# Deformable convolution on one core: x loads on SyncE, statistics from band 4 on, one of four tile copies by a transfer, another order of stores and loads at the head

## The chip, the cores and the metric

The kernel runs on one core of one Trainium2 chip. The metric is the device time of one execution in microseconds (us), the median of several runs. The engines are named as in the profile: PE is TensorE, DVE is VectorE, ACT is ScalarE, POOL is GpSimd, SP is SyncE, which here only issues transfers (DMAs). ACT, POOL and SP each have their own queue of transfers.

## The reference, cut to what matters

The input x is 8 samples x 128 channels x 64 x 64. Layer 0 adds to x a deformable 3x3 convolution of its group-normalised copy (each of 9 taps reads the image at a position shifted by a learned offset, bilinearly, times a sigmoid mask), followed by batch normalisation over all samples and a relu. Layer 1 adds a mixture of four 3x3 convolutions, of which each sample chooses two, and a shared one. The change lies in layer 0 alone.

```python
om  = conv3x3(gn(x), off_w) + off_b            # 27 planes: 9 y offsets, 9 x offsets, 9 masks
val = bilinear(gn(x), grid + off) * sigmoid(om[:, 18:])
y   = einsum('bckhw,ock->bohw', val, w) + b    # 9 taps, 128 channels
x   = x + relu(batchnorm(y) * gamma + beta)
...
x   = x + moe_conv3x3(gn(x), top-2 of 4 experts) + shared_conv3x3(gn(x))
```

## The kernel before, in words

**Sampling as matmuls.** Every sample is cut into 8 horizontal bands of 8 rows (NB = 8); band g = 8b + j is band j of sample b, 64 bands in all. Inside a band the pixels are gathered in small tiles of 4 columns, and the samples at the shifted positions are made by TensorE: a tile of pixels (transposed, `xt`) times a sparse weight matrix s. An element of s is a tent in x times a tent in y, so `weights(n)` (L846) makes s on VectorE as a product of a table of x weights (`xwts`) and a table of y weights (`ywts`). The numbers of s run on: n = 5g + q, with five sample groups q a band.

**The tables.** For every sample `tables(b)` makes, from the statistics of the image (`statistics`, eight `bn_stats`, L303), the normalised image (`pad`, L343 on ACT and L347 on DVE), the offset convolution (combinations of rows in the combo buffers, L421 and L423, and matmuls, L456), the offsets in rows and columns through HBM (stores L523 and L530, loads L568 and L554), tents on ACT (L639, L643), masks on DVE (L676), and tables of x distances and y weights that are stored to HBM (`store_x` L594, `store_y` L666). It is a generator: each call of `tick()` puts the next few instructions into the program, and `pause(n)` lets n ticks pass. So the table work for sample b+2 is woven, tick by tick, into the bands of samples b and b+1. Statistics run in band 5 of sample b (`j == NB - 3`), the tables start there at tap 7, the combos fall in bands 6 to 0, the offsets are loaded and turned into tents in bands 1 to 4.

**One band** (the loop over g):
- For q = 0 to 4: `weights` for the group three ahead (AHEAD = 3), then `sample`: 12 matmuls into PSUM (L862) and one copy by ACT (L872). So in q = 0 the fourth s of the same band is made, in q = 1 the fifth, in q = 2 to 4 the first three of the next band. With q = 2 and 3 POOL issues the eight y loads of band g+2 (L725), which wait for the last s that read the buffer.
- Then the nine taps ("parts" 0 to 8) of the convolution of band g-1 (L911), with other work between them: at parts 0 and 1 transposes for band g+2 (L807, ACT copies L810); at part 2 the x load of band g+3 (two transfers of 576 KB together, L744, on POOL); at parts 1, 3, 5 and 7 `spread` of band g+2, which turns x distances into weights: absolute values on ACT (L763, L766) at parts 1 and 3, clips on DVE (L769) at parts 5 and 7; at part 4 `pick` for g+3 (L778).
- `share` (L821) copies the transposed tiles of band g+2 shifted by one for the other parity, in four pieces of 32 rows: pieces 0 and 2 by DVE at parts 2 and 3, pieces 1 and 3 by ACT at parts 4 and 6. So the tiles of a band are made two bands ahead.
- `put_off` adds after the second group the statistics of y (L991) and copies at the edge (L888 to L895).

**What orders the work.** Instructions of one engine run in program order. PE, DVE, ACT, POOL and SP wait for each other only where data or a buffer asks for it: `xwts` has three buffers, `ywts` two, s four, the PSUM tiles pq three, and the tiles pt, pm, pv and pc share one PSUM buffer.

**The head.** Sample 0's tables are made before the first band; they end with the stores of x distances and y weights, the loads for band 0, the statistics of sample 1 and the first spread.

The loop around the change:

```python
made, means_of = later, iter(())
...
if odd == 0 and part == 2:
    load_x(g + 3, nc.gpsimd)
...
if odd == 0 and part in (2, 3, 4, 6):
    piece = {2: 0, 3: 2, 4: 1, 6: 3}[part]
    share(g + 2, piece, MOVES[piece])
```

Of the kernel before, what the change touches and what calls it, by code (L numbers as in the profile page):

```python
# [17 lines left out]
H = W = 64  # L18
# [22 lines left out]
NR = 2 * REACH + 1  # L41
T = 4
# [3 lines left out]
NROW = H // T  # L46
NB = NROW // 2
# [18 lines left out]
def deform_moe_conv(  # L66
# [113 lines left out]
    def dense():  # L180

        with ExitStack() as st:
# [126 lines left out]
            def tables(b):  # L309
# [233 lines left out]
                )  # L543
                yield from pause(16)
                by_row = rowwise[b].rearrange("(t k u) h w -> k h t u w", t=3, k=3)
# [31 lines left out]
                if b == 0:  # L577
                    for piece in range(4):
                        share(1, piece, MOVES[piece])
                yield from pause((50, 9)[b] if b < 2 else 35)  # L580

# [114 lines left out]
                distances_x()  # L696
                store_x(0, 2, nc.gpsimd)
                load_x(0, nc.gpsimd)
                for i in (0, 1, 2):
# [6 lines left out]
                for k in range(Q):  # L706
                    for h in range(2):
                        load_y(0, k, (nc.sync, nc.gpsimd, nc.scalar, nc.gpsimd)[k % 4], (h,))
                for _ in statistics(1):
                    pass  # L710
                for tiles in ((NCOL, NCOL + 1), (0, 3), (3, 9), (9, NCOL)):
                    spread(0, tiles)
                store_x(2, 6, nc.gpsimd)
                store_x(6, NROW, nc.sync)
                store_y(0, NR, slice(4 * T, H))

# [108 lines left out]

            MOVES = (nc.vector.tensor_copy, nc.scalar.copy) * 2

            def width(q):
                return GT * T + 2 * (q in (0, NGR - 1))

            def weights(n, engine=nc.vector):

                if n >= len(bands) * NGR:
                    return
                g, q = divmod(n, NGR)
                s = a6.tile([P, M, 3 * (GT * T + 2)], F32, name="s")
                by_x = x_wts[g % 3].rearrange("p (c m x) -> p m c x", m=M, x=3)
                by_y = y_wts[g % 2].rearrange("p r y w x -> p (r y) w x")
                main = GT * T * q
                parts = [(2 * (q == 0), main, 2 + main, GT * T)]  # L840
                if q == 0:
                    parts.append((0, NCOL * T, 0, 2))
                if q == NGR - 1:
                    parts.append((GT * T, NCOL * T + 2, W - 2, 2))
                for at, c, w, k in parts:
                    engine.tensor_tensor(  # L846
                        s[:, :, 3 * at : 3 * (at + k)].rearrange("p m (c x) -> p m c x", x=3),
                        by_x[:, :, c : c + k], by_y[:, :, w : w + k], ALU.mult,
                    )
                ss[n] = s  # L850
# [114 lines left out]
            for n in range(AHEAD):  # L965
                weights(n, nc.vector if n < AHEAD - 1 else nc.gpsimd)
            HALVES = (0, EVEN), (EVEN, NCOL + 1)
# [32 lines left out]
            for g in range(len(bands) + 1):  # L1000
                b, j = bands[g] if g < len(bands) else (B, 0)
                if j == NB - 3:
                    means_of = statistics(b + 2)
# [3 lines left out]
                for q in range(NGR):  # L1007
                    if g < len(bands):
                        if g or q + AHEAD < NGR:
                            weights(g * NGR + q + AHEAD)  # L1010
                        sample(g * NGR + q)
                        if q in (2, 3):
                            for k in range(T * (q - 2), T * (q - 1)):
                                load_y(g + 2, k, nc.gpsimd)
                    if g == 0 and q == 1:
                        for _ in range(2):
                            while next(later) != BLOCK:
                                pass
                        for _ in range(8):
                            next(later)  # L1020
                    if q == 1:
                        put_off()
                taps = conv(g - 1) if g else iter(())
                twice = 2 if g and bands[g - 1][1] == NB - 1 else 1
                for done, _ in enumerate(taps):
                    part, odd = divmod(done, twice)
                    if odd == 0 and part in PIXELS:
                        next(turned, None)
                    if odd == 0 and part == 2:
                        load_x(g + 3, nc.gpsimd)  # L1030
                    if odd == 0 and part in SPREAD:
# [29 lines left out]
                if g == 0:  # L1061
                    for piece in range(4):
                        share(2, piece, MOVES[piece])
                    load_x(3, nc.gpsimd)
                    pick(3)
# [3 lines left out]
                    spread(2)  # L1069
                if g == 4:  # L1070
                    quad_weights()
# [603 lines left out]
```

## Time and profile before

| what | value |
|---|---|
| median of 3 runs | 1478.61 us (1473.09 to 1479.34) |
| the profiled execution | 1472.76 us, span 1471.0 us |
| mean granted TensorE clock | 0.96 |
| PE busy | 1300.3 us (88% of the span) |
| DVE busy | 1064.9 us (72%) |
| ACT busy | 902.7 us (61%) |
| POOL busy | 448.5 us (30%) |
| software DMA queue (POOL's) | 137.50 MB, 44.6% of the 16 engines' span |
| hardware DMA queue (SP's and ACT's) | 87.97 MB, 20.4% |

Layer 0 takes about the first 1085 us of the span. In the profile a row of a group is: line, engine, operation, output <- inputs, sizes, count, busy time, mean duration, and the idle time just before with what ended it. In a timeline a row is start, busy time, engine, line, operation; a bracket at its end is the idle time before it and its releaser. In a table of windows the columns are the window, its length, busy time (and count) of PE, PEld, DVE, ACT, POOL, the granted clock (PEclk), the share of the DMA engines and GB/s. Where bands are named below, a band begins with its first sample matmul and ends with the next band's.

Lengths of bands, read from the PE timeline in this way (us):

| sample | band 4 | band 5 | band 6 | band 7 | band 0 of the next |
|---|---|---|---|---|---|
| 1 | 18.6 | 16.1 | 13.1 | 17.2 | 21.0 |
| 2 | 17.5 | 17.9 | 13.1 | 17.2 | 21.9 |
| 3 | 14.7 | 18.5 | 14.7 | 17.2 | 21.1 |
| 4 | 18.9 | 17.9 | 13.1 | 17.2 | 21.0 |
| 5 | 21.8 | 17.9 | 13.1 | 17.2 | 21.1 |
| 6 | 13.9 | 14.9 | 13.1 | 13.1 | 18.6 |

Bands 1 to 3 of these samples take 12.2 to 13.1 us. Sample 0 is longer: its bands 0 to 7 take 17.2, 24.9, 23.4, 14.1, 13.1, 26.6, 14.8 and 30.0 us.

### The profile page before, as it was taken

What the parts mean: (1) busy time and instruction counts of PE and PEld (TensorE: products, weight loads), DVE (VectorE), ACT (ScalarE), POOL (GpSimd) and SP (SyncE); (2) the same over time, 40 slices, a digit from 0 to 9 for tenths busy, and PEclk for the clock granted to TensorE, in tenths of its full rate; (3) what the DMA queues carried; (4) which work ended last, traced back from release to release, by engine and by line L of the source; (5) the groups of instructions that cost most, each with busy time, mean ns of one, the idle gap of its engine ahead of it and who ended that gap; (6) DMA issues with size and microseconds to landing.
All of it is one profiled execution on the core that took longest, in us unless ns stands there. A gap on an engine that the chain in (4) does not pass through costs nothing.

```text
span 1471.0 us, 21219 instructions
## 1 busy us (share of the span) xinstructions
PE 1300.3 (88%) x7561; PEld 740.1 (50%) x7561; DVE 1064.9 (72%) x2113; ACT 902.7 (61%) x1183; POOL 448.5 (30%) x755
## 2 busy tenths in 40 slices
PE   4169779989989998998998999989975999999998
PEld 1144446555655665664565566556642444444443
DVE  5657687689668868967875896756628877878882
ACT  2365766887787688689777868977723333231320
POOL 6353232343343343343343334344212101011000
PEclk9579989999999999999999999999997999999999
DMA  4485755976887598598778778777618544565411
GB/s 147 106 184 122 164 131 133 208 180 140 182 184 181 129 211 186 126 189 182 171 145 174 179 168 170 174 194 181 175 32 243 140 120 135 149 171 158 114 44 60
DMA packets 146342, 227.33 MB, mean 155 GB/s; under 512 B 100574, under 2 KB 103802, under 8 KB 135986
## 3 DMA queue, kind: packets, MB, share of 16 engines
q0 software_dynamic: 79472, 137.50, 44.6%
q1 hardware_dynamic: 66618, 87.97, 20.4%
q8 instruction: 62, 1.02, 0.3%
q14 instruction: 54, 0.44, 0.1%
q10 hardware_dynamic: 136, 0.41, 0.1%
HBM read 180.23 MB, written 45.35 MB: 153 GB/s over the span
## 4 chain that ended last, share of the span: by engine, by line
PE 46%; DMA 16%; DVE 15%; issue 10%; ACT 9%; POOL 3%; SPq 1%; DVEq 0%; ACTq 0%; POOLq 0%
PE py L911 16%; PE pc L1587 14%; PE pq L862 10%; DMA ywts<-taby 5%; DMA xwts<-tabx 4%; DVE s L846 3%; PE pt L807 2%; PE pc L456 2%; DVE combo L423 2%; ACT xwts L763 2%; DVE stats L303 2%; POOL ywts L725 2%; DVE xwts L769 2%; DVE combo L421 1%; DMA pad<-in_x_dram 1%
## 5 line engine op out<-in xcount | busy, mean ns | idle before, releaser
L911 PE MATMUL py<-samples,dw_sb 128*128 128x512 f32 (+3 forms) x1296 | 553.4, 561 | 7.2 <-ACT y L919 5.4
L725 POOL DMA_DIRECT2D ywts<-taby x512 | 296.6, 600 | 527.3 <-DVE s L846 440.9
L862 PE MATMUL pq<-s,xt 64*128 64x144 f32 (+1 forms) x3840 | 294.1, 307 | 90.8 <-DVE s L846 50.6
L862 PEld LDWEIGHTS pq<-s,xt 64*128 64x128 f32 x3840 | 264.5, 195 | 136.0 <-ACT samples L872 55.3
L911 PEld LDWEIGHTS py<-samples,dw_sb 128*128 128x128 f32 x1296 | 228.2, 189 | 206.7 <-issue 178.1
L872 ACT COPY samples<-pq 128x864 f32<-128x864 f32 (+1 forms) x320 | 282.5, 972 | 53.0 <-PE pq L862 52.1
L846 DVE TENSOR_TENSOR s<-xwts,ywts 128x72 f32<-128x72 f32 (+1 forms) x447 | 199.5, 500 | 68.6 <-PE pq L862 59.2
L1587 PE MATMUL pc<-v,u 128*128 128x512 f32 x384 | 174.2, 600 | 6.3 <-DVE v L1494 6.3
L1587 PE MATMUL pc<-v,wmix 128*128 128x512 f32 x384 | 173.2, 596 | 0.0
L763 ACT ACTIVATE xwts<-xwts,place 128x1152 f32<-128x1152 f32 (+3 forms) x132 | 153.0, 1163 | 23.4 <-DMA xwts<-tabx 21.5
L821 DVE COPY xt<-xt 32x896 f32<-32x896 f32 x126 | 78.5, 623 | 114.2 <-ACT xt L810 113.2
L1565 ACT ACTIVATE t<-pc,bmix 128x512 f32<-128x512 f32 x32 | 22.0, 687 | 187.5 <-PE pc L1587 99.1
L769 DVE TENSOR_SCALAR xwts<-xwts 128x1152 f32<-128x1152 f32 (+2 forms) x128 | 92.9, 755 | 39.9 <-ACT xwts L763 26.3
L821 ACT COPY xt<-xt 32x896 f32<-32x896 f32 x126 | 118.0, 936 | 2.4
L1587 PEld LDWEIGHTS pc<-v,u 128*128 128x128 f32 x384 | 71.8, 191 | 93.0 <-issue 83.1
L1587 PEld LDWEIGHTS pc<-v,wmix 128*128 128x128 f32 x384 | 72.0, 189 | 90.8 <-issue 88.9
L810 ACT COPY xt<-pt 128x512 f32<-128x512 f32 (+1 forms) x130 | 76.1, 586 | 62.2 <-PE pt L807 60.5
L807 PEld LDWEIGHTS pt<-ident,picked 128*128 128x128 f32 x512 | 60.2, 142 | 76.5 <-ACT xt L810 39.0
L744 POOL DMA_DIRECT2D xwts<-tabx x128 | 79.1, 630 | 52.0 <-DMA ywts<-taby 20.5
L807 PE MATMUL pt<-ident,picked 128*128 128x128 f32 x512 | 79.8, 279 | 5.3 <-ACT xt L810 2.9
L919 ACT ACTIVATE y<-py,db_sb 128x512 f32<-128x512 f32 (+3 forms) x72 | 45.7, 635 | 57.3 <-PE py L911 50.0
L778 DVE COPY picked<-pad 128x512 f32<-128x512 f32 x128 | 72.1, 605 | 1.5 <-PE pt L807 0.8
(205 smaller groups left out, 1154.0 us busy)
## 6 DMA issues: line engine op xcount, KB each, us to landing
xwts<-tabx POOLq DMA_DIRECT2D x128, 576.0 KB, 9.4
pad<-in_x_dram SPq DMA_DIRECT2D x36, 512.0 KB
ywts<-taby POOLq DMA_DIRECT2D x126, 144.0 KB, 7.9
out_dram<-yo SPq DMA_DIRECT2D x32, 512.0 KB
ywts<-taby POOLq DMA_DIRECT2D x126, 108.0 KB, 7.6
yd<-y SPq DMA_DIRECT2D x48, 256.0 KB
ywts<-taby POOLq DMA_DIRECT2D x128, 72.0 KB, 7.2
pad<-yd SPq DMA_DIRECT2D x16, 512.0 KB
```

The costliest lines, as they stand in the source:

```text
L725: engine.dma_start(out=y_wts[g % 2][HALF * h + k : HALF * (h + n) : Q, first : last + 1].rearrange("p r a b c -> p (r a b c)"), in_=bass.A ...
L744: engine.dma_start(out=x_wts[g % 3][HALF * h : HALF * h + HALF], in_=bass.AP(tensor=x_table[b].tensor, offset=x_table[b].offset + (2 * j + ...
L763: nc.scalar.activation(some, some, AF.Abs, bias=columns[side])
L769: nc.vector.tensor_scalar(some, some, -1.0, 0.0, ALU.add, ALU.min)
L807: nc.tensor.transpose(pt[:, c - c0], one.rearrange("p h x y -> p (h x y)"), ident)
L810: nc.scalar.copy(xts[g][:, c0 : c0 + n], pt[:, 0:n])
L821: move(out=xts[g][rows, EVEN:].rearrange("p c n -> p (c n)"), in_=xts[g][rows, 1 - side : EVEN - side].rearrange("p c n -> p (c n)"),)
L846: engine.tensor_tensor(s[:, :, 3 * at : 3 * (at + k)].rearrange("p m (c x) -> p m c x", x=3), by_x[:, :, c : c + k], by_y[:, :, w : w + k] ...
L862: nc.tensor.matmul(by_m[:, h, :, at : at + k], lhsT=xts[g][rows, c // 2 + EVEN * (c % 2)], rhs=s[rows, :, at : at + k], start=True, stop=True,
L872: nc.scalar.copy(bass.AP(tensor=one.tensor, offset=one.offset + first, ap=[list(one.ap[0]), [M * PLANE, 2], [PLANE, M], [WB + 1, 3], [1, w ...
L911: nc.tensor.matmul(py, lhsT=dw_sb[:, 3 * (2 - yy) + 2 - xx], rhs=samples[g % 2][:, m : m + 3 * n - 2 : 3, xx, 1 : W + 1], start=(i == 0), ...
L1587: nc.tensor.matmul(pc, lhsT=us[j][:, kx], rhs=vs[g][:, rows, kx : kx + W], start=(kx == 0), stop=(kx == 2),)
```

## The change

- The x load of band g+3 goes out on SP instead of POOL, in the third sample group (q = 2) of band g instead of after the second tap; for g = 5 at the second tap as before, but on SP. 122 of the 128 x transfers move.
- Statistics of sample b+2: one `bn_stats` at each of parts 5 to 8 of band 4 and two at each of parts 0 and 1 of band 5, instead of two at each of parts 0, 1, 2 and 4 of band 5. The tables of b+2 start at part 4 of band 5 instead of part 7 (for b = 0 at part 7 as before), so what follows comes three taps earlier.
- The pieces of `share`: DVE's two move from parts 2 and 3 to parts 6 and 8; one of ACT's stays at part 4; the other becomes a transfer on SP at part 2 (32 x 896 elements of 4 bytes). So 63 of the copies of ACT become transfers.
- At the head the table of x distances is stored in other pieces: rows 2 to 3 on POOL ahead of the first x load, the rest and the rest of the y table on SP ahead of the statistics of sample 1. The third s of the head is made by DVE instead of POOL. Weights of the offset convolution (`quad_weights`) are made after band 5 instead of 4.
- Two pauses of the early tables change: 8 instead of 16 for sample 1 ahead of the loads of offsets, 17 instead of 9 after them.

```diff
-                yield from pause(16)
+                yield from pause(8 if b == 1 else 16)
...
-                yield from pause((50, 9)[b] if b < 2 else 35)
+                yield from pause((50, 17)[b] if b < 2 else 35)
...
                 store_x(0, 2, nc.gpsimd)
+                store_x(2, 4, nc.gpsimd)
                 load_x(0, nc.gpsimd)
...
+                store_y(0, NR, slice(4 * T, H))
+                store_x(4, NROW, nc.sync)
                 for _ in statistics(1):
                     pass
                 for tiles in ((NCOL, NCOL + 1), (0, 3), (3, 9), (9, NCOL)):
                     spread(0, tiles)
-                store_x(2, 6, nc.gpsimd)
-                store_x(6, NROW, nc.sync)
-                store_y(0, NR, slice(4 * T, H))
...
-            MOVES = (nc.vector.tensor_copy, nc.scalar.copy) * 2
+            MOVES = (
+                nc.vector.tensor_copy, nc.scalar.copy, nc.vector.tensor_copy, nc.sync.dma_start
+            )
...
-                weights(n, nc.vector if n < AHEAD - 1 else nc.gpsimd)
+                weights(n)
...
+            SHARE = 6, 4, 8, 2
...
-                if j == NB - 3:
+                if j == NB - 4:
                     means_of = statistics(b + 2)
...
+                        if q == 2 and g != NB - 3:
+                            load_x(g + 3, nc.sync)
...
-                    if odd == 0 and part == 2:
-                        load_x(g + 3, nc.gpsimd)
+                    if odd == 0 and part == 2 and g == NB - 3:
+                        load_x(g + 3, nc.sync)
...
-                    if odd == 0 and part in (2, 3, 4, 6):
-                        piece = {2: 0, 3: 2, 4: 1, 6: 3}[part]
+                    if odd == 0 and part in SHARE:
+                        piece = SHARE.index(part)
                         share(g + 2, piece, MOVES[piece])
-                    if odd == 0 and j == NB - 3 and part in (0, 1, 2, 4):
+                    if odd == 0 and j == NB - 4 and part > 4:
+                        next(means_of, None)
+                    if odd == 0 and j == NB - 3 and part < 2:
                         for _ in range(2):
                             next(means_of, None)
-                    if odd == 0 and j == NB - 3 and part == 7 and b + 2 < B:
+                    if odd == 0 and j == NB - 3 and part == (4 if b else 7) and b + 2 < B:
                         for _ in made:
                             pass
                         asked, made = True, tables(b + 2)
...
-                if g == 4:
+                if g == 5:
                     quad_weights()
```

More of the change, by code (lines that the diff above doesn't have):

```diff
@@ L824, in share, with weights @@
                 )
-            MOVES = (nc.vector.tensor_copy, nc.scalar.copy) * 2
+            MOVES = (
+                nc.vector.tensor_copy, nc.scalar.copy, nc.vector.tensor_copy, nc.sync.dma_start
+            )
             def width(q):
                 return GT * T + 2 * (q in (0, NGR - 1))
-            def weights(n, engine=nc.vector):
+            def weights(n):
                 if n >= len(bands) * NGR:
@@ L845, in weights @@
                 for at, c, w, k in parts:
-                    engine.tensor_tensor(
+                    nc.vector.tensor_tensor(
                         s[:, :, 3 * at : 3 * (at + k)].rearrange("p m (c x) -> p m c x", x=3),
@@ L1063, in dense @@
                         share(2, piece, MOVES[piece])
-                    load_x(3, nc.gpsimd)
                     pick(3)
```

## The prediction

> **What bounds the kernel now.** I read the page's busy shares first, then the chain, then the waits of VectorE (DVE), then the timelines of the bands where TensorE (PE) stands still.
>
> ```profile
> PE 1300.3 (88%) x7561; PEld 740.1 (50%) x7561; DVE 1064.9 (72%) x2113; ACT 902.7 (61%) x1183; POOL 448.5 (30%) x755
> PE 46%; DMA 16%; DVE 15%; issue 10%; ACT 9%; POOL 3%; SPq 1%; DVEq 0%; ACTq 0%; POOLq 0%
> DVE xt L821 <- ACT xt L810: 113.2, 44, 5.3
> xwts<-tabx POOLq DMA_DIRECT2D x128, 576.0 KB, 9.4
> ```
>
> PE is the bound, but the average hides the stages. A band with no extra work takes 13.1 us and PE never idles in it. The bands that are longer are those in which the next sample's tables are made, and what ends PE's wait there is nearly always the fourth product s of the band (call it s3): it is issued at the head of the band, behind everything that VectorE still holds from the band before, and PE needs it 2.6 us later, after three sample groups. Two causes make s3 late. The first is a late x transfer, here at band 4 of sample 4 (PE, ACT, DVE timelines, then PE clock by windows: length, busy times, PEclk, DMA share, GB/s):
>
> ```profile
> 665.44 2.60 PE L862 MATMUL pq<-s,xt 64*128 64x216 f32 x36
> 671.89 2.37 PE L862 MATMUL pq<-s,xt 64*128 64x144 f32 x22 [3.85 <-ACT samples L872]
> 663.26 1.25 ACT L763 ACTIVATE xwts<-xwts,place 128x1152 f32<-128x1152 f32 x1 [3.26 <-DMA xwts<-tabx]
> 671.06 1.26 DVE L846 TENSOR_TENSOR s<-xwts,ywts 128x432 f32<-128x432 f32 x3
> 672.00:678.00 6.00, 6.00 (x35) 3.76 (x36) 3.46 (x10) 4.27 (x6) 4.91 (x9) 0.72 0.62 151
> ```
>
> ACT waits 3.26 us for x, clips and tents slide, s3 starts at 671.06 where PE wanted it at 668.0, and after 3.85 us of idle PE runs at a mean granted clock of 0.72 for 6 us. The second cause is VectorE's own queue, here sample 0's band 7 (six combos and two clips in the 8.3 us ahead of s3):
>
> ```profile
> 205.40 2.60 PE L862 MATMUL pq<-s,xt 64*128 64x216 f32 x36
> 213.62 3.49 PE L862 MATMUL pq<-s,xt 64*128 64x144 f32 x24 [5.62 <-DVE s L846]
> 210.60 2.35 DVE L421 TENSOR_TENSOR combo<-pad 128x1024 f32<-128x1024 f32 x2
> ```
>
> In the regular samples that queue is nearly full but in time. Band 7 of sample 3 starts at 588.73:
>
> ```profile
> 586.76 1.12 ACT L763 ACTIVATE xwts<-xwts,place 128x1008 f32<-128x1008 f32 x1
> 588.61 1.89 ACT L821 COPY xt<-xt 32x896 f32<-32x896 f32 x2
> 587.91 1.43 DVE L769 TENSOR_SCALAR xwts<-xwts 128x1152 f32<-128x1152 f32 x2 [0.84 <-ACT xwts L763]
> 589.25 1.22 DVE L423 SCALAR_TENSOR_TENSOR combo<-pad 128x1024 f32<-128x1024 f32 x1
> 590.39 1.27 DVE L846 TENSOR_TENSOR s<-xwts,ywts 128x432 f32<-128x432 f32 x3
> 592.18 1.93 PE L862 MATMUL pq<-s,xt 64*128 64x144 f32 x24 [0.85 <-ACT samples L872]
> ```
>
> The clips wait for ACT's last x activation (ends 587.88), one combo follows, and PE loses only 0.85 us.
>
> **What the skill says.** "TensorE: Matmul & The Clock Gate", Part 1: The HAM clock gate: PE falls to half its clock after at least one idle window of about 3.4 us. The trace agrees in kind (0.72 above) and gives the price: band 4 of sample 2 takes 17.5 us with 2.5 idle, of sample 1 18.6 with 3.6, so 1.9 above 13.1 plus idle in both, while 1.2 idle (sample 3) cost 0.4. The same page, "Architectural detail": ACT and VectorE are strict FIFO; the 113.2 us of "xt" waits are time in which everything behind them stood. "Trainium Kernel Development and Optimization", Key Constraints: transfers of SP, ACT and POOL share 16 engines; several issuers only save issue time. So moving x to SP speeds no bytes: the DMA share is 0.98 to 1.05 from 652 to 672 as it is; only an earlier start helps.
>
> **The change part by part.**
>
> *x loads.* 122 of 128 leave POOL, where they stand behind the y loads that wait for VectorE's s, and go at the third group, some 4 to 7 us before the old place (after the second tap). They wait for s4 of the same group. Behind them on SP are only stores of y, pad loads, stores of offset tables and the new xt transfers; none is needed within a band. ACT's idle for x in band 3 was 1.9, 0.6, 3.3 and 5.2 us in samples 2 to 5: with loads that start 4 to 7 us earlier nearly all of it goes. What is late next is VectorE, because four statistics (2.4 us) come into band 4 and its two xt copies (1.24) now stand right before s3. By sample 4: with x at 660.0, clips, tents (2.2), xt copy and last mask put s3's end at 668.3 against 668.0, so 3.5 of 3.85 and the cold clock of 1.9 are saved; but s3 of band 5 is now some 4 us late instead of 1.5, with cold clock (+2.5 +1.5); two psum waits (0.9 and 1.2) in band 5 go since statistics end earlier. 36.8 becomes 33.3. Likewise samples 2, 3, 5: 35.4, 33.2, 39.7 become about 33.2, 32.5, 33.7. Together -12. Sample 1's 3.6 us come from its own tents on ACT, not from x, and it gets the late s3 too: +1.
>
> *Head and sample 0.* Two more x stores go ahead of the x load and the early third of the tables is stored first. Band 1's idle of 3.4 us (x lands at 91.8) with its cold clock, 1.9: -5. Sample 0's band 5 idles 7.5 us: VectorE waits 4.4 us for a transfer of row offsets, which now is asked for eight steps earlier, and the 1.6 us of quad weights leave; four statistics and xt come: 2.7 left, -5. The xt copies ahead of s3 cost 1.2 in band 2 and 1.1 in band 7. Sum -8 (between -5 and -11).
>
> *Sample 7's first band* (18.6 us, 1.2 and 2.7 idle, x late): -3.
>
> *One xt copy as a transfer.* ACT loses 63 x 0.94 us. ACT is not the bound, and in band 6 the copies stand behind the activation that the clips wait for (lines above), so this frees nothing there. The trace has no such transfer (112 KB): "DMA: Bandwidth & Descriptors", Anatomy of one DMA, gives 2.0 us and bytes by 436e3, an estimate of 2.3; the page's rows of 72 to 144 KB took 7.2 to 7.9. I take 7.5; either is hidden, as xt is needed a band (13.1 us) later. 7 MB more is 3% of 227 MB.
>
> *xt copies moved and tables three steps earlier: bands 6, 7, 0.* This is the loss. In band 6, from 587.9 (fixed by ACT as above) VectorE now has before s3: two clips 1.43, two xt 1.24, three combos 3.66 (two of them came after s3 before), s3 0.6: done at 594.8, needed at 591.3: 3.5 us idle where 0.85 was. Its early wait for xt is gone, but the time freed lies in the middle of band 6, where nothing else is ready. In band 7: 594.8, then 0.7 + 1.0 + 1.8 (statistics of y, edges, four s), five combos 6.1, two picks 1.1, a clip 0.7, two small 0.84, combos and xt alternating 1.2 + 0.6 + 1.2, clip 0.7, combos 2.4, xt 0.6, s3 0.6: about 614.4. PE, itself 2.6 later, needs it at 611.1: 3.3 idle where 0.9 was. Band 0 then has three combos (3.7) less and 20.2 us of PE work, so nothing is left over. Idle +2.6 +2.4 = +5.0. Each stall is of the size that cost 1.9 us of cold clock above; I take 1.1, as the window does not always fall in it: +2.2. So +7.2 in each of five windows (samples 1 to 5), +36; without cold clock +25.
>
> **Sum,** against the profiled execution (1472.8, span 1471.0): 1472.8 - 12 + 1 - 8 - 3 + 36 = 1486.8. That run stands 5.9 below the median of 1478.6 and at the low end of the runs; what lengthens the others isn't shown, and if it is late x it goes with the change, so I add nothing: 1487.
>
> **Rivals.**
> 1. *Queue, but no cold clock.* Idle of 3.3 to 3.5 us scattered over two windows leaves the clock up: 1472.8 - 12 + 1 - 8 - 3 + 25 = 1476. For it: after 1.5 us of idle band 5 of sample 2 loses at most 0.9 (17.9 less 3.6 idle, beside 14.9 less 1.5 in sample 6). Against: 2.5 us did cost 1.9.
> 2. *Queue absorbed, faster.* The place is band 6: if ACT ends its x work about 2.5 us earlier (x early, less copying), the clips start at 585.4 and s3 of band 7 ends by 592.3, 1.0 late. It decides when that activation ends before 585.5; then band 7 is as before and only band 0's +2.4 is left, without cold clock: 12 in all; sample 1's +1 stays out: 1472.8 - 12 - 8 - 3 + 12 = 1462. For it: VectorE loses 113 us of waiting. Against: ACT's list in band 6 gains a pad operation (0.73) ahead of that activation.
> 3. *The change doesn't do what it says.* x waits on SP behind a store whose producer is late, so band 4 stays as it is: 1487 + 12 = 1499. Against: SP's share in the chain is 1%.
>
> **Chances.** Main case 0.38 (own range 1479 to 1497), rival 3 0.07, rival 1 0.23, rival 2 0.32. About 0.5% (7.4 us) is what a measurement tells from no change: faster 0.32, same 0.23, slower 0.45. Rival 2 reaches down to 1450 if the x gain is 20; I leave out its lower third and the upper part of rival 3: 1456 to 1500.
>
> **What would show it.** Right: PE idle of 3 to 4 us at the heads of bands 7 and 0 of samples 1 to 5 "<- DVE s" with PEclk below 1 after it; no ACT wait for x in band 3; idle at the head of band 5. Wrong: s3 of band 7 ends within 3.5 us of its start (rival 2), or ACT still waits for x in band 3 (rival 3).

## The result, and the profile after

The changed kernel takes 1537.45 us (median of 4 runs, 1536.58 to 1543.0), the kernel before 1478.16 us (median of 4). The ratio is 1.0416, 95% interval 1.0381 to 1.045, which is 61 us of 1478 (the two medians differ by 59.3). The forecast was slower by some 9 us, with 1456 to 1500 as its range. The sign was right, the size was missed by a factor of about seven, and the time lies outside the range.

The page of the changed kernel (profiled execution 1537.18 us, span 1535.3 us, mean clock 0.936), its busy shares and its chain:

```profile
PE 1329.4 (87%) x7561; PEld 761.6 (50%) x7561; DVE 1060.8 (69%) x2114; ACT 845.5 (55%) x1120; POOL 370.0 (24%) x632
PE 52%; DVE 14%; DMA 14%; issue 8%; ACT 6%; SPq 3%; POOL 2%; DVEq 0%; POOLq 0%; ACTq 0%
```

PE runs the same 7561 matmuls, but they are busy for 29.1 us more (1329.4 less 1300.3): that is the lower granted clock (0.936 on average against 0.96). Idle time of PE inside the 64 bands, summed from the PE timelines, grew from 85 to 119 us. Together, 29 and 34 are the 63 us that layer 0 became longer. ACT has 57 us of work less and DVE 4; the kernel is no faster for either.

By stage, from the PE timelines as in the table of before (us, idle of PE in brackets; the whole of layer 0 is 63 longer, the span 64):

```
stage                               before          after       change   forecast
head and sample 0                  71.3+164.1     71.9+165.8     +2.3      -8
bands 4 and 5, samples 1 to 5     179.8 (34.0)   192.0 (41.3)   +12.2     -11
bands 7, samples 1 to 5            86.0  (4.3)   111.7 (18.2)   +25.7  }
bands 0, samples 2 to 6           106.1  (5.3)   128.3 (18.4)   +22.2  }  +36
band 0, sample 7                   18.6  (3.9)    15.7  (1.4)    -2.9      -3
other bands                                                      +3.1       0
```

The forecasts sum to +14, the measured changes to +63. Of the 49 us between them 23 lie in bands 4 and 5, 12 in bands 7 and 0, and 10 in the head and sample 0.

What VectorE and ACT wait for in the changed kernel (waits of DVE, then of ACT: us in total, times, longest):

```profile
DVE xwts L769 <- ACT xwts L763: 103.9, 33, 4.5
DVE s L848 <- DMA ywts<-taby: 65.0, 19, 8.1
DVE xt L821 <- ACT xt L810: 12.3, 2, 7.1
```

```profile
ACT xwts L763 <- DMA xwts<-tabx: 12.9, 6, 4.1
```

The 113.2 us that VectorE stood before its tile copies are down to 12.3, and ACT's wait for x fell from 21.5 to 12.9 us. In their place VectorE waits 103.9 us at the clips (before 26.3) and 65.0 us for y weights (before 1.5, at the same instruction). Of the 101 us that went at the copies, 78 came back at the clips, another instruction of the same engine; the y waits are new.

Band 7 of sample 2 (starts at 488.40), DVE timeline and then PE timeline, shows the stall as it was forecast:

```profile
487.59 0.76 DVE L769 TENSOR_SCALAR xwts<-xwts 128x1152 f32<-128x1152 f32 x1 [4.10 <-ACT xwts L763]
488.27 0.61 DVE L821 COPY xt<-xt 32x896 f32<-32x896 f32 x1
488.80 0.74 DVE L769 TENSOR_SCALAR xwts<-xwts 128x1152 f32<-128x1152 f32 x1
489.47 1.21 DVE L423 SCALAR_TENSOR_TENSOR combo<-pad 128x1024 f32<-128x1024 f32 x1
490.69 0.62 DVE L821 COPY xt<-xt 32x896 f32<-32x896 f32 x1
491.32 1.22 DVE L423 SCALAR_TENSOR_TENSOR combo<-pad 128x1024 f32<-128x1024 f32 x1
492.58 1.22 DVE L421 TENSOR_TENSOR combo<-combo 128x1024 f32<-128x1024 f32 x1
493.72 1.26 DVE L848 TENSOR_TENSOR s<-xwts,ywts 128x432 f32<-128x432 f32 x3
```

```profile
488.40 2.60 PE L864 MATMUL pq<-s,xt 64*128 64x216 f32 x36
494.47 3.49 PE L864 MATMUL pq<-s,xt 64*128 64x144 f32 x24 [3.47 <-DVE s L848]
```

VectorE waits 4.10 us for ACT's last x activation, then works through two clips, two tile copies and three combos without a gap, and the fourth s starts 6.1 us after the first clip. PE stands for 3.47 us. The next rows are windows of this band and of the band 0 after it (length, busy of PE, PEld, DVE, ACT, POOL, then clock, DMA share, GB/s):

```profile
491.00:494.50 3.50, 0.03 (x3) 0.06 (x2) 3.45 (x5) 1.22 (x2) 0.00 (x0) 0.88 0.00 0
494.50:498.00 3.50, 3.50 (x25) 2.98 (x25) 3.47 (x11) 0.91 (x2) 1.75 (x3) 0.50 0.51 129
498.00:502.00 4.00, 4.00 (x13) 2.21 (x14) 3.97 (x5) 1.62 (x2) 2.58 (x5) 0.69 0.95 194
516.30:520.00 3.70, 3.63 (x27) 2.64 (x28) 3.46 (x10) 1.95 (x2) 2.82 (x6) 0.67 0.50 125
```

After 3.5 us of idle PE has half its clock for 3.5 us and 0.69 of it for 4 more; after 2.75 us at the head of band 0, 0.67. The first stall costs nearly as much again after it has ended (half of 3.5 us and 0.31 of 4 us, some 3.0 us); over the ten stalls of bands 7 and 0 it is 2.1 us each, as worked out below.

### The profile page after: what moved, and what is told of

It reads as the page before. It is cut to its first block, busy times and chain, and to the rows that moved or that the text cites. A ratio compares the mean times of both kernels' runs of the same rounds, so it can differ in the third digit from the quotient of the medians.

```text
span 1535.3 us, 21237 instructions
## 1 busy us (share of the span) xinstructions
PE 1329.4 (87%) x7561; PEld 761.6 (50%) x7561; DVE 1060.8 (69%) x2114; ACT 845.5 (55%) x1120; POOL 370.0 (24%) x632
## 4 chain that ended last, share of the span: by engine, by line
PE 52%; DVE 14%; DMA 14%; issue 8%; ACT 6%; SPq 3%; POOL 2%; DVEq 0%; POOLq 0%; ACTq 0%
PE py L913 19%; PE pc L1593 13%; PE pq L864 12%; PE pt L807 3%; PE pc L456 3%; DVE combo L423 3%; DMA ywts<-taby 2%; DMA pad<-in_x_dram 2%; DMA xt<-xt 2%; SPq L554 2%; DMA xwts<-tabx 2%; DVE xt L821 2%; DMA yd<-y 2%; DVE xwts L769 1%; DVE s L848 1%
## 5 line engine op out<-in xcount | busy, mean ns | idle before, releaser
L913 PE MATMUL py<-samples,dw_sb 128*128 128x512 f32 (+3 forms) x1296 | 565.1, 570 | 10.6 <-ACT y L921 8.8
L864 PE MATMUL pq<-s,xt 64*128 64x144 f32 (+1 forms) x3840 | 311.6, 319 | 129.8 <-DVE s L848 118.0
L864 PEld LDWEIGHTS pq<-s,xt 64*128 64x128 f32 x3840 | 279.3, 205 | 178.6 <-issue 110.1
L848 DVE TENSOR_TENSOR s<-xwts,ywts 128x432 f32<-128x432 f32 (+1 forms) x448 | 198.3, 497 | 102.1 <-DMA ywts<-taby 65.0
L769 DVE TENSOR_SCALAR xwts<-xwts 128x1152 f32<-128x1152 f32 (+2 forms) x128 | 95.9, 749 | 108.3 <-ACT xwts L763 103.9
L763 ACT ACTIVATE xwts<-xwts,place 128x1152 f32<-128x1152 f32 (+3 forms) x132 | 153.0, 1163 | 13.0 <-DMA xwts<-tabx 12.9
L821 DVE COPY xt<-xt 32x896 f32<-32x896 f32 x126 | 77.2, 612 | 13.2 <-ACT xt L810 12.3
L821 ACT COPY xt<-xt 32x896 f32<-32x896 f32 x63 | 59.1, 938 | 1.5
L994 DVE BATCH_NORM_STATS2 ystats<-y 128x6 f32<-128x512 f32 (+3 forms) x72 | 44.6, 627 | 20.0 <-ACT y L921 20.0
## 6 DMA issues: line engine op xcount, KB each, us to landing
ywts<-taby POOLq DMA_DIRECT2D x126, 144.0 KB, 10.1
```

The lines of the kernel that those rows point to most:

```text
L763: nc.scalar.activation(some, some, AF.Abs, bias=columns[side])
L769: nc.vector.tensor_scalar(some, some, -1.0, 0.0, ALU.add, ALU.min)
L821: move(out=xts[g][rows, EVEN:].rearrange("p c n -> p (c n)"), in_=xts[g][rows, 1 - side : EVEN - side].rearrange("p c n -> p (c n)"),)
L848: nc.vector.tensor_tensor(s[:, :, 3 * at : 3 * (at + k)].rearrange("p m (c x) -> p m c x", x=3), by_x[:, :, c : c + k], by_y[:, :, w : w + ...
L864: nc.tensor.matmul(by_m[:, h, :, at : at + k], lhsT=xts[g][rows, c // 2 + EVEN * (c % 2)], rhs=s[rows, :, at : at + k], start=True, stop=True,
L913: nc.tensor.matmul(py, lhsT=dw_sb[:, 3 * (2 - yy) + 2 - xx], rhs=samples[g % 2][:, m : m + 3 * n - 2 : 3, xx, 1 : W + 1], start=(i == 0), ...
```

## The experiments

The kernels ran on several chips, each beside the kernel before on the same chip, whose medians there were 1466.6 to 1475.4 us. So each is given by its ratio to the kernel before, with the 95% interval in brackets, and "+17" means that ratio less one, times 1478. The changed kernel itself is +61. Lengths of stages are read from one profiled execution of each version, and they scatter: with the tables back at part 7 (number 4), an edit that leaves sample 0 as it is, sample 0 took 172.1 us against 165.8, and single bands 4 differ by up to 3.5 us where an edit changes nothing in them. Bands 7 and 0 repeat far better.

First, two theories. "VectorE's list": the fourth s is late since copies and combos stand ahead of it on VectorE in bands 6 and 7. "x ahead of y": the x loads on SP take the engines while the y loads, which are needed sooner, are under way.

**1. x back after the second tap, still on SP.**

```diff
-                        if q == 2 and g != NB - 3:
+                        if q == 2 and not g:
                             load_x(g + 3, nc.sync)
...
-                    if odd == 0 and part == 2 and g == NB - 3:
+                    if odd == 0 and part == 2:
                         load_x(g + 3, nc.sync)
```

> The changed kernel with every x load back after the second tap (band 0 apart), still on SP. Theory 'x ahead of y': in the changed kernel the 1.15 MB of x goes out beside or ahead of the y loads of the same band, which are needed sooner, and VectorE waits 65 us (19 times) for y weights; with x behind y these waits fall below 15 us, bands 4 and 5 of samples 1 to 5 lose some 20 us together, and the time is 1511 to 1522. Rival 'VectorE's list alone': the y waits lie in slack that the list would have filled anyway; bands 7 and 0 keep their +48, bands 4 and 5 do not move, 1531 to 1541. Both leave bands 7 and 0 at about 22 and 25.7 us.

Measured 1.0428 (1.0383 to 1.0473), +63, where the theory expected 1511 to 1522 us. The y waits stayed at 69.4 us (20 times), and bands 7 and 0 hardly moved (109.0 and 128.3 us). But this run does not refute the theory, for its edit moved x in the program and not in time. SP only issues transfers, and nothing on SP waits for the second tap. Here are SP's timelines for bands 2 and 3 of sample 2, first of the changed kernel (the bands begin at 412.78 and 425.89), then of this run (412.29 and 425.40):

```profile
418.22 1.15 SPq L744 DMA_DIRECT2D xwts<-tabx  x2
434.28 1.17 SPq L744 DMA_DIRECT2D xwts<-tabx  x2
```

```profile
417.54 1.25 SPq L744 DMA_DIRECT2D xwts<-tabx  x2
433.67 1.12 SPq L744 DMA_DIRECT2D xwts<-tabx  x2
```

In both kernels x goes out 5.3 to 5.4 us after the start of the first band and 8.3 to 8.4 us after that of the second; over all bands the median difference is 0.0 us.

**2. x on SP alone, in the kernel before.**

```diff
+                        if q == 2 and g != NB - 3:
+                            load_x(g + 3, nc.sync)
...
-                    if odd == 0 and part == 2:
-                        load_x(g + 3, nc.gpsimd)
+                    if odd == 0 and part == 2 and g == NB - 3:
+                        load_x(g + 3, nc.sync)
...
-                    load_x(3, nc.gpsimd)
```

> The kernel before with only the x loads moved: SP, third sample group (band 5 of sample 0 at its second tap). Theory 'x ahead of y': VectorE waits for y by some 40 to 60 us where it waited 1.5, bands 3 to 5 grow, 1488 to 1503; bands 7 and 0 stay at 17.2 and 21. Rival 'early x helps': the late x of bands 3 and 4 goes and y stays in time, 1462 to 1474.

1.0113 (1.007 to 1.0157), +17, at the lower end of what the theory expected. VectorE waits 49.2 us for y (19 times); sample 0 grew from 164.1 to 171.5 and bands 3 and 4 of sample 1 from 31.7 to 42.1. The late x did go: band 4 of samples 4 and 5 fell from 18.9 and 21.8 to 15.0 and 17.4, band 0 of sample 7 from 18.6 to 15.7. The move pays where it was meant to, and more is lost elsewhere: samples 0 and 1 grew by 7.4 and 10.9 us, and all the rest together came out about as before.

**3. All x back on POOL, in the changed kernel** (with band 0's own load, as before).

```diff
-                        if q == 2 and g != NB - 3:
-                            load_x(g + 3, nc.sync)
...
-                    if odd == 0 and part == 2 and g == NB - 3:
-                        load_x(g + 3, nc.sync)
+                    if odd == 0 and part == 2:
+                        load_x(g + 3, nc.gpsimd)
...
+                    load_x(3, nc.gpsimd)
```

> The changed kernel with all x loads back on POOL after the second tap, in the queue of the y loads. With SP after the second tap the y waits of VectorE stayed at 69 us, so the earlier issue is not their cause. Theory 'two queues': x on SP shares the 16 engines with y, x on POOL follows it; y waits fall below 15 us, y lands after some 7.5 us again, and the time is 12 to 22 us below the changed kernel's distance to before: +38 to +50 us over before. Rival 'other transfers (table loads, xt) delay y': y waits stay at 40 to 70 us and the time at +55 to +68 over before.

1.0446 (1.0392 to 1.0499), +66: the y waits did what the theory said, the time (+38 to +50) did not. Its transfers (KB each, median us to landing) and waits of DVE:

```profile
xwts<-tabx POOLq DMA_DIRECT2D x128, 576.0 KB, 10.0
ywts<-taby POOLq DMA_DIRECT2D x126, 144.0 KB, 7.4
```

```profile
DVE xwts L769 <- DMA ywts<-taby: 15.2, 3, 5.7
DVE s L848 <- DMA ywts<-taby: 13.2, 3, 5.4
```

The large y transfers land after 7.4 us again, against 10.1 with x on SP, and the wait of s for them falls from 65.0 to 13.2. So x on SP is what makes y late. Band 2 of sample 2 shows how, first in the changed kernel (POOL, SP, DVE, then a window), then with x on POOL (the band begins at 402.15):

```profile
415.03 5.30 POOL L725 DMA_DIRECT2D ywts<-taby  x8 [7.85 <-DVE s L848]
418.22 1.15 SPq L744 DMA_DIRECT2D xwts<-tabx  x2
435.08 1.80 DVE L848 TENSOR_TENSOR s<-xwts,ywts 128x432 f32<-128x432 f32 x4 [5.88 <-DMA ywts<-taby]
420.00:426.00 6.00, 6.00 (x16) 2.37 (x15) 3.01 (x5) 3.87 (x6) 0.34 (x1) 1.00 1.04 241
```

```profile
404.42 3.92 POOL L725 DMA_DIRECT2D ywts<-taby  x7 [5.81 <-DVE s L848]
409.28 0.56 POOL L725 DMA_DIRECT2D ywts<-taby  x1 [0.94 <-DMA xwts<-tabx]
411.48 1.07 POOL L744 DMA_DIRECT2D xwts<-tabx  x2 [1.63 <-DMA ywts<-taby]
```

On SP x goes out among the eight y loads, the DMA engines are full (share 1.04), the slowest of these loads takes 15.6 us to land, and in the next band s waits 5.88 us for y. On POOL x follows the last y load, and no load of the eight takes more than 8.0 us. Over all bands the first x transfer goes out 5.6 us after the band's start on SP and 10.6 us on POOL (medians). So the move changes queue and time together, and no run tells one from the other. But the total did not fall (the profiled execution has a span of 1530.8 us against 1535.3, and the intervals overlap). Against the changed kernel, bands 4 became 10.6 us shorter and sample 0 3.8; band 0 of sample 7 became 7.2 longer (22.9), band 6 of that sample 4.3. With the rest of the change in place, the choice of queue decides which table is late and hardly the time. "Two queues" explains the y waits and not the 61 us.

**4. Where the loss in bands 7 and 0 comes from.** The tile pieces back at their parts (the transfer at 6), and the tables back to part 7, in the changed kernel:

```diff
-            SHARE = 6, 4, 8, 2
+            SHARE = 2, 4, 3, 6
```

> The changed kernel with the pieces of the shifted tiles at the parts of before (VectorE's at 2 and 3, ACT's at 4, the transfer at 6). Theory 'VectorE's list': two copies of 0.62 leave the stretch ahead of the fourth product, so bands 7 and 0 lose 1.2 of idle each and a part of their cold clock: 2 to 4 us in each of ten bands less, 1505 to 1518. Rival 'only the three moved combos count': VectorE waits for the transposed tiles again (over 80 us) and nothing is won, 1531 to 1541.

```diff
-                    ... part == (4 if b else 7) and b + 2 < B:
+                    ... part == 7 and b + 2 < B:
```

> The changed kernel with all tables starting at part 7 of band 5, as before. Theory 'VectorE's list': the three combos go back behind the fourth product; band 7 loses 2.4 of idle and band 0 most of its idle, with their cold clock, so some 7 us in each of five windows and 1498 to 1507. Rival 'the start does not matter, the xt copies do': less than 10 us, 1527 to 1538.

1.027 (1.0224 to 1.0316), +40, and 1.0257 (1.0205 to 1.0309), +38. Each alone takes off 21 to 23 us. With the pieces back, bands 7 (samples 1 to 5) fall from 111.7 to 99.4 and bands 0 from 128.3 to 117.7, and bands 5 from 101.7 to 89.3; with the tables back, bands 7 and 0 fall to 86.9 and 117.4, and bands 4 and 5 together stay (192.4). In bands 7 and 0 the tables so give the 7 us a window that were expected; the total is less than the expected 30 to 39 as sample 0 and bands 5 came out 6.3 and 5.3 us longer in this execution.

Both of these edits together:

> The changed kernel with the tile pieces at the parts of before and all tables from part 7 on; x on SP, the early statistics, the transfer and the head stay. Theory: the two losses in bands 7 and 0 are one queue and nearly all of it goes (bands 7 at 17.2 to 18.5, bands 0 at 21 to 22), what is left is x on SP: +10 to +22 us over before. Rival 'they add, without the queue': each undoing gave 20, both together 40, the same sum; but if they overlap (either alone frees the queue) only 25 to 30 come back, +30 to +38.

1.0128 (1.0071 to 1.0185), +19. Bands 7 are at 81.3 with no idle at all, less than before, bands 0 at 109.8. So copies and tables together make 42 of the 61 us. In the total the two parts add; in bands 7 they don't (12 and 25 us alone, 30 together). The sum of the totals is also what two unconnected losses would give; that both work through VectorE's list is read from the timeline of band 7 above. Bands 4 and 5, though, are at 201.8 in this run.

**5. Each part alone, in the kernel before.** The tile pieces (places and transfer), then the same with all four still copies (the second change of the diff alone), then VectorE's two copies alone:

```diff
-            MOVES = (nc.vector.tensor_copy, nc.scalar.copy) * 2
+            MOVES = (
+                nc.vector.tensor_copy, nc.scalar.copy, nc.vector.tensor_copy, nc.sync.dma_start
+            )
...
-                    if odd == 0 and part in (2, 3, 4, 6):
-                        piece = {2: 0, 3: 2, 4: 1, 6: 3}[part]
+                    if odd == 0 and part in (2, 4, 6, 8):
+                        piece = {6: 0, 8: 2, 4: 1, 2: 3}[part]
```

> The kernel before with only the tile pieces changed: VectorE's at parts 6 and 8, one of ACT's a transfer at part 2. Theory 'VectorE's list': 1.24 us more ahead of the fourth product, bands 7 idle 2.1 instead of 0.9 and bands 0 some 2 instead of 0.9, with cold clock in part: bands 7 some 19 to 20, bands 0 some 23: +12 to +25 us over before. Rival 'the wait for tiles that goes pays for it': within 6 us of before.

1.024 (1.0191 to 1.029), +35, a miss in size and place. Expected were +12 to +25 in bands 7 and 0. Bands 7 hardly moved (86.0 to 86.8); bands 0 of samples 2 to 6 grew by 7.7 us, that of sample 7 by 7.9, sample 0 by 7.3 and bands 5 of samples 1 to 5 by 8.5.

> The kernel before with the tile pieces at the changed kernel's parts (VectorE's at 6 and 8, ACT's at 4 and 2), all still copies. With the transfer in it the same gave +36 us over before. Theory 'VectorE's list': the two copies ahead of the fourth product are what costs: +25 to +40 over before. Rival 'the transfer': the move alone gives +0 to +12, the transfer and what it takes from the 16 engines the rest.

1.0421 (1.0346 to 1.0495), +62, far above both. In this version one of ACT's copies stands at part 2, ahead of the activation at part 3 that the clips wait for, and VectorE waits 166.6 us at the clips. It does not tell what VectorE's copies cost, so it was split:

```diff
-                    if odd == 0 and part in (2, 3, 4, 6):
-                        piece = {2: 0, 3: 2, 4: 1, 6: 3}[part]
+                    for piece in {4: (1,), 6: (0, 3), 8: (2,)}.get(part, ()) if odd == 0 else ():
                         share(g + 2, piece, MOVES[piece])
```

> The kernel before with only VectorE's two tile copies moved to parts 6 and 8; ACT's stay at 4 and 6. In the run with all four moved, one of ACT's stood at part 2, ahead of the activation that the clips wait for. Theory 'VectorE's list': the two copies ahead of the fourth product cost +20 to +32 over before (the share change less the transfer gave +25). Rival 'ACT's copy at part 2 was the cost': +0 to +12.

1.0184 (1.0138 to 1.023), +27, as expected. The waits of DVE in this run:

```profile
DVE xwts L769 <- ACT xwts L763: 140.7, 36, 7.1
DVE xt L821 <- ACT xt L810: 10.5, 2, 5.3
```

103 us of waiting at the copies went (113.2 to 10.5) and 114 us came at the clips (26.3 to 140.7). So the waits at the copies had cost little: VectorE would have stood at the clips instead. The work of the copies, once done before that wait, now comes after it, ahead of the fourth s. Two instructions of 0.62 us a band cost 27 us so, most of it in bands 5 and 0 (each some 9 us over samples 1 to 7); bands 7 have room for them (86.7 us) as long as the tables start late. The difference of 35 between the two runs in which all pieces are still copies is what 0.94 us of ACT a band ahead of the activation costs.

The transfer alone (`MOVES` as in the diff above, the places of before, so at part 6), and the transfer with ACT's copy kept. The second was meant to add traffic alone, but the transfer writes the same rows after the copy, so PE's tiles then also wait for it:

```diff
                         share(g + 2, piece, MOVES[piece])
+                        if piece == 3:
+                            share(g + 2, piece, nc.sync.dma_start)
```

> The kernel before with ACT's last tile copy (part 6) as a transfer on SP, nothing else. Theory 'VectorE's list': the transfer is hidden and costs nothing: -4 to +4 us over before. Rival 'the transfer': +15 to +30, with x and y landing later.

1.0072 (1.0047 to 1.0098), +11, between the two expectations.

> The kernel before with ACT's last tile copy kept and the same piece sent once more by a transfer on SP after it: only the traffic of the transfer is added. Theory 'the transfer takes x's time on the engines': +8 to +18 over before, ACT waits for x by over 35 us. Rival 'what ACT does with its freed time': -3 to +4.

1.0108 (1.0077 to 1.0139), +16. The transfer isn't hidden. ACT's wait for x is 44.5 us in the first, 31.2 in the second, against 21.5 (the second less than expected). PE itself waits for the transfer for 7.7 us (3 times) in the first and 33.1 us (5 times) in the second; band 4 of sample 3 in the second shows why (PE timeline, then ACT's and SP's; a DMA row's time is SP's time to issue):

```profile
550.34 0.88 PE L862 MATMUL pq<-s,xt 64*128 64x216 f32 x6
558.90 6.77 PE L862 MATMUL pq<-s,xt 64*128 64x144 f32 x54 [7.67 <-DMA xt<-xt]
```

```profile
535.42 1.89 ACT L821 COPY xt<-xt 32x896 f32<-32x896 f32 x2
536.21 12.20 SPq L554 DMA_DIRECT2D combo<-colwise  x5
548.52 0.46 SPq L281 DMA_DIRECT2D pad<-in_x_dram  x1
549.09 0.60 SPq L821 DMA_DIRECT2D xt<-xt  x1
```

Five loads of turned offsets (L554) hold SP's queue for 12.2 us; the tile piece for the band that begins at 550.3 is issued at 549.1, 11.8 us after ACT's copy of it ended (537.3). As bands 4 grew by 21 us in this run, its +16 says more of late issue than of traffic. In the first run ACT's missing copy does buy something: bands 7 fall from 86.0 to 81.3 us, without idle. Bands 0 lose it again (106.1 to 110.4).

The tables alone, and with the statistics (as in the diff of the change):

```diff
-                    ... part == 7 and b + 2 < B:
+                    ... part == (4 if b else 7) and b + 2 < B:
```

> The kernel before with only the tables of b+2 starting at part 4 of band 5; the statistics stay in band 5. With early statistics too it was +30 over before, +12 of it in bands 7 and +15 in bands 0. Theory 'the three combos': +18 to +32, bands 7 at 18.5 to 20, bands 0 at 23 to 26. Rival 'the early statistics carry a part': +5 to +15, with bands 7 and 0 less long.

1.0334 (1.0275 to 1.0392), +49.

> The kernel before with only the early statistics (from band 4 on) and the tables of b+2 from part 4 on. Theory 'VectorE's list': the three combos go ahead of the fourth product of bands 7 and 0: 2.4 us more idle there and cold clock, with two psum waits less in band 5: +10 to +25 over before. Rival 'only together with the moved copies': the list has room for one of the two, -6 to +5.

1.0207 (1.0155 to 1.0259), +31. Both are more than expected. The early start of the tables costs 49, and early statistics give 18 of it back: with late ones PE waits 10.5 us (5 times) for the mean that the tables begin with, where it waited 5.1 before, and bands 5 of samples 1 to 5 are at 101.4 against 88.6. In both runs bands 7 of samples 1 to 6 are at 110.4 (99.1 before).

**6. The head, and versions that might beat both.** The head alone, with all its edits from the diff of the change (stores, pauses, third s, weights of the offset convolution):

> The kernel before with only the head changed (stores and loads, pauses of the early tables, third s on VectorE, weights of the offset convolution after band 5). By the prediction sample 0 and the head win 5 to 11 us, 10 with the tile copies left out. Rival: the stall of band 1 goes, another takes its place in bands 0 to 2 and 5, as the changed kernel's profile hints: within 4 us of before.

0.994 (0.992 to 0.9961), -9: as forecast. Band 1 of sample 0 falls from 24.9 to 19.6, its idle from 5.0 to 1.6; band 5 from 26.6 to 24.6.

The head with ACT's last piece as a transfer at part 6:

> The kernel before with the changed head and ACT's last tile copy as a transfer: a candidate that beats both. The head alone gave -9 us. If the transfer is hidden: -7 to -14 us; if ACT's freed 0.94 us a band is worth something where ACT's activations are late: -14 to -18; if the transfer delays x and y: 0 to +15.

1.0106 (1.0042 to 1.0169), +16: missed. The parts alone sum to +2; against the head alone bands 4 and 5 grew most (99.8 and 102.6 to 111.1 and 109.6). What the other 14 are is open; the intervals leave 6 to 25 for the whole.

The head with x early on SP from sample 2 on:

```diff
+                        if q == 2 and b > 1:
+                            load_x(g + 3, nc.sync)
...
-                    if odd == 0 and part == 2:
+                    if odd == 0 and part == 2 and b < 2:
                         load_x(g + 3, nc.gpsimd)
```

> The kernel before with the changed head, and x loads early on SP only in the bands of samples 2 to 7. x early on SP cost most in samples 0 and 1 (some 17 us by the profile), and in the others its gain (late x of bands 4 of samples 4 and 5 and of sample 7) about paid for the y waits. Theory: -8 to -16 us from before, level with or a little below the head alone (-9). Rival 'two queues cost everywhere': -4 to +6.

0.9935 (0.9899 to 0.9972), -10, level with the head alone: x on SP is worth about nothing after sample 1 (VectorE's y waits are 21.5 us here) and costs in samples 0 and 1.

The head with the early statistics:

```diff
-                if j == NB - 3:
+                if j == NB - 4:
                     means_of = statistics(b + 2)
...
-                    if odd == 0 and j == NB - 3 and part in (0, 1, 2, 4):
+                    if odd == 0 and j == NB - 4 and part > 4:
+                        next(means_of, None)
+                    if odd == 0 and j == NB - 3 and part < 2:
```

> The kernel before with the changed head and the early statistics (from band 4 on), the tables from part 7 of band 5 as before: the one part of the change that no run has shown without the early tables. With the tables early, early statistics took 19 us off (tables alone +49, with statistics +30), but there they take away a wait that the early tables make. Theory: here they move 2.4 us from band 5 to band 4, where the fourth product of band 5 stands behind them; the psum waits of band 5 (0.9 and 1.2) go instead: -12 to +2 us from before, that is -3 to +11 from the head alone (-9). Rival 'statistics are worth most of the 19 anywhere': -20 to -30 from before.

1.0006 (0.9983 to 1.0028), +1. So early statistics without early tables cost some 9 us beside the head; their 18 above only mend what the early tables break.

## Why the prediction was wrong, point by point

**Bands 7 and 0: mechanism and place right, one term too small.** Idle was forecast at 3.5 and 3.3 us a stall; the profile has 3.5 in bands 7 (4.3 once) and 3.7 in bands 0, of which 2.8 at the head. The cold clock was put at 1.1 us a stall. Over the five windows the loss is 47.9 us; idle makes 27.0 of it, (18.2 + 18.4) less (4.3 + 5.3), so 20.9 is clock, 2.1 a stall. The profile before had the number, 1.9 for idles of 2.5 and 3.6; taking little more than half of it, "as the window does not always fall in it", was the error, worth some 10 us. The clock also fell to half after idles of 2.47 us (before, from 420.3 to 423.6) and 2.75 us, shorter than the window of about 3.4 us that the prediction quotes, so a stall shorter than that is not free. Taking away either half of the list brought back 21 to 23 us, both 42.

**The x loads: the step that failed.** The forecast was that bands 4 and 5 of samples 1 to 5 become 11 us shorter; they became 12.2 us longer. "Behind them on SP are only stores of y, pad loads, ... none is needed within a band" looked at what stands behind x on SP. It put at nothing what x does to the y loads on POOL, which run at the same time. Before, x stood behind y in POOL's queue; on SP it went out 3.4 us sooner (median, where 4 to 7 were forecast), in most bands before the last y load. The y transfers of 144 KB then landed after 10.1 us where they had taken 7.9, and VectorE waited 65.0 us for them. With x back on POOL both went (7.4 and 13.2 us).

The gain itself came in part. Of ACT's waits for x in band 3, the prediction's own sign, those of samples 2, 3 and 5 are gone, that of sample 4 is 2.5 us instead of 3.3, and sample 1 has a new one of 3.9 us. The late x of sample 7's band 0 went as forecast (-2.9).

That x on SP costs by itself is shown (+17 alone, in samples 0 and 1). That it costs 23 us of the 61 is not: with x back on POOL in the changed kernel, bands 4 and 5 became only 7.4 us shorter (184.6), and the total stayed, since x was late again in sample 7. With the tile copies back bands 5 returned to 89.3 us from 101.7 (88.2 before), though bands 4 grew by 4.7. So in bands 5 the longer list of VectorE is the likely cause; this was not taken apart further.

**The transfer: forecast 0, measured +11 alone.** The step reckoned with a landing of 7.5 us, taken from transfers that POOL issues, and a need 13 us later, and "7 MB more is 3%". ACT's wait for x doubled beside the transfer (21.5 to 44.5 us). With the copy kept, the transfer itself was issued late, behind SP's 12.2 us of loads, and PE waited until 558.90, 9.8 us after the issue. The step priced the transfer from its size and left out what stands ahead of it on SP. "This frees nothing there" was wrong too: bands 7 lost their 0.86 us of idle. In the changed kernel the transfer goes out at part 2 and PE does not wait for it, so the 11 cannot simply be carried over; how much of it is traffic and how much order was not taken apart.

**The head: right alone, lost in company.** -8 was forecast, -9 measured alone. In the changed kernel head and sample 0 are +2.3: the moved pieces alone add 7.3 to sample 0 (171.4), which the forecast put at 2.3, and x on SP alone adds 7.4, which it left out. Both lie near the scatter of sample 0, so this account is likely and not shown.

**The rivals.** "Queue absorbed, faster" is refuted: ACT's last activation in band 6 of sample 2 ends at 487.55 (VectorE's clip follows at 487.59), 0.85 us ahead of band 7; before, in sample 3, it was 0.85 too (587.88 and 588.73). "Queue, but no cold clock" is refuted by 29 us of PE time for the same matmuls. Of "x waits on SP" the half about SP's queue was right: in band 3 of sample 2 the loads of turned offsets (L554) hold SP, and x goes out 8.4 us after the band's start. But they are loads and not a store, and ACT waited less for x than before (12.9 us against 21.5), so this was not the loss.

**The sum.** The parts alone are x +17, pieces +35, statistics and tables +31, head -9: +74, against +61. So in total they overlap. In bands 7 of samples 1 to 5 it is the other way round: the pieces alone add 0.8 us and statistics with tables 11.3, but all together add 25.7, as each alone still finds room there. The forecast counted this rightly, with copies and combos in one list; it summed the other gains and losses as if each stage kept its own slack, and its range had no case in which a gain turned into a loss. Not explained is how the 12.2 us in bands 4 and 5 split between y, statistics and copies: undoing the copies left these bands at 184.3, undoing copies and tables at 201.8.

## What to carry to other kernels

When a load moves to another queue, ask of the old queue whose transfers it used to follow, and of the new one what issues ahead of it and for how long. Here the order inside POOL's queue had kept x behind y, and a move that "speeds no bytes" took that away. Moving the call in the program does not move the transfer in time if nothing on the issuing engine waits there: check the issue time in the timeline before reading such a run. An in-order engine's wait early in its list can be cover for work; removing the wait by moving that work to the end of the list puts it in front of whatever the bottleneck needs next. Price a stall of the bottleneck with the full loss of clock that the profile already shows after stalls of that length. Test parts together as well as alone, since slack that covers each alone may not cover both.

## What the runs showed that was not expected

- Idle of 3.47 us on PE (band 7 of sample 2) is followed by a granted clock of 0.50 from 493.7 to 500.5, some 6.8 us; idle of 2.75 us (the band 0 after it) by 0.50 from 517.6 to 520.9, some 3.3 us.
- Five loads of turned offsets hold SP for 12.1 us in the changed kernel (421.09 to 433.15) and for 12.2 us in the run with both copy and transfer, single ones up to 5.9 us in the changed kernel.
- One ACT copy of 0.94 us a band, at part 2 instead of 6 and so ahead of the activation that the clips wait for, made 35 us (+62 against +27). What an instruction costs depends on its place.
